# A four-layer graph kernel: neighbours centred in their sorting networks, networks in place, and small sums moved to TensorE

## The chip, the core and the metric

The kernel runs on one NeuronCore of a Trainium2 chip. A core has a matrix engine (TensorE, PE in the profile), a vector engine (VectorE, DVE), an activation engine (ScalarE, ACT), a general engine (GpSimd, POOL) and a queue engine for plain DMA transfers (SyncE, SP). They run in parallel and wait for each other through semaphores. The metric is the time on the device in microseconds (us), the median of several runs. The profile is one execution taken apart.

## The reference

Sixteen graphs of 1024 nodes with 64 features each; an adjacency matrix with random weights, about 16 neighbours to a node. Four layers, each a pre-normalised residual step `x = x + layer(relu(layernorm(x)))`:

```python
# layer 0:  h + messages, a tanh network
messages = einsum('bij,bjh->bih', adjacency, h)
dh = tanh(concat([h, messages]) @ W1 + b1) @ W2 + b2
# layer 1:  weighted mean over neighbours and self
A = edges + eye;  out = (A @ nodes) / A.sum(2)
# layer 2:  per node and channel, quantiles over the neighbours
nb = (adj > 0) & ~eye                     # rows with more than 10 neighbours lose some of them
removed = nb & do_dil & ((rank + 1) % skip == 0)
valid = where(removed | removed.T, 0, adj_with_self_loops) > 0
sv = sort(where(valid, x[:, None], big), axis=2);  m = valid.sum(-1)
for tau, wt in zip([.25, .5, .75], [.25, .5, .25]):
    pos = tau * (m - 1)                   # interpolated between sv[floor(pos)] and sv[ceil(pos)]
    agg += wt * quantile
y = relu((x + agg) @ W1 + b1) @ W2 + b2
# layer 3:  mean message
out = (A @ X / A.sum(1)) @ W_neighbors + X @ W_self + bias
```

## The kernel before

A graph's nodes lie on the 128 partitions in eight blocks. For layer 2 the kernel orders the 1024 nodes by their number of neighbours, m, cuts them into eight blocks of 128 and treats these in five groups (`GROUPS`): block 0 alone, block 1 alone, then three pairs. Every group has a capacity `cap` (38, 20, 18, 16, 13 places) and a lower bound `low` for m. For a group GpSimd gathers, place by place, one neighbour's feature row for every node of a block: one indirect DMA of 128 rows of 64 floats (line 1243, tile `raw`). How many places of a block are gathered whole stands in `PLACES`; the few rows of block 0 with more neighbours get theirs through three packed gathers (line 1224). Places beyond the neighbours are filled with zeros. VectorE then sorts each node's list per channel with an odd-even merge network: every step is a minimum or a maximum of two strided views, many comparators in one instruction (line 1285). The results of one layer go from `raw` to a second tile `other` or back, so that no step overwrites its own input; the home of every place is followed in `_program`, and comparators whose sources or targets lie in different tiles need instructions of their own. Comparators that no wanted place needs are dropped. At last each wanted place is multiplied by a weight per node (zero for places that a node's quantiles don't touch) and added up in `agg` (lines 1306 and 1308).

The rest of one graph: `adjacency` (transposes the matrix by TensorE, finds which neighbours go, ranks the nodes by m, writes keys to DRAM), `neighbour_lists` (gathers keys in node order on GpSimd, line 1064, and takes the neighbours in eights with MAX8, lines 1079 to 1095; then `index` and the weights), `layers` (layers 0 and 1 and the normalised input of layer 2), `gathers`, `sorts`, and `tail` (brings `agg` back to node order on GpSimd, line 1328, layer 2's two matrix products, layer 3).

A second, general path stands behind a test at the end and isn't taken with these inputs. These six are Python generators, and a small planner at build time interleaves them over the sixteen graphs. It keeps a clock for each engine (`clk`), advanced by rough costs that the generators state; a generator that yields a time is resumed when VectorE's clock has reached it; among those that are due the first in the list goes, so `sorts` comes last. The order on each engine is fixed by this; on the chip, semaphores hold each instruction until its inputs are there. GpSimd's gathers are charged 1.27 us each. `gathers(b)` for group k may start once `sort(b-1, k)` is done, since `raw` has one buffer for each group.

GpSimd is kept from running ahead of VectorE's plan by marks and gates. The planner lets VectorE write a mark (a one-element memset, line 889) whenever 4 us of its clock have gone by; before every fourth place of a group, GpSimd copies the latest mark (line 896, `gate`), and so waits until VectorE has passed it.

Small sums are VectorE's: the biases b02, b22 and b3 (lines 1154, 1344, 1363), the residuals (1163, 1365), the self term and the one of layer 1's denominator (1185, 1188) and the sum in front of layer 2's products (1332), each a 128x512 operation on one graph's nodes except for line 1185.

Of the kernel before, what the change touches and what calls it, by code (L numbers as in the profile page):

```python
# [17 lines left out]
P = 128  # L18
C = 64
# [18 lines left out]
GROUPS = [(0, 1, 38, 17), (1, 1, 20, 15), (2, 2, 18, 12), (4, 2, 16, 10), (6, 2, 13, 1)]  # L38

E_ID, E_ONE, E_CAP, E_LOW, E_CN, E_Q, E_END = 0, 128, 256, 264, 272, 280, 320  # L40
# [3 lines left out]
PLACES = [22, 20, 18, 17, 16, 14, 13, 12]  # L44
PACKS = [(22, 2, 64), (24, 4, 32), (28, 10, 12)]
# [3 lines left out]
def _span(cap, low):  # L49

    return (low - 1) // 4, -(-3 * (cap - 1) // 4)


def _network(cap, low):
# [16 lines left out]
    lo, hi = _span(cap, low)  # L71
    live, kept = set(range(lo, hi + 1)), []
    for layer in reversed(layers):
        layer = [(i, j, i in live, j in live) for i, j in layer if j < cap and (i in live or j in live)]
        for i, j, _, _ in layer:
            live |= {i, j}
        if layer:
            kept.append(layer)
# [3 lines left out]
def _patterns(items):  # L82


    left, out = set(items), []
    while left:
        best = None
        for x in sorted(left):
            steps = sorted({(y[2] - x[2], y[3] - x[3]) for y in left if y[:2] == x[:2] and y > x})

            def run(start, v):
                row = [start]
                while (z := (*x[:2], row[-1][2] + v[0], row[-1][3] + v[1])) in left:
                    row.append(z)
                return row

            for v in [None, *steps]:
                row = [x] if v is None else run(x, v)
                if best is None or len(row) > len(best[0]):
                    best = (row, x, [(len(row), *(v or (0, 0)))])  # L100
                for w in steps if v else []:
                    cover, m = list(row), 1
                    while all((z := (*x[:2], r[2] + m * w[0], r[3] + m * w[1])) in left and z not in cover
                              for r in row):
                        cover += [(*x[:2], r[2] + m * w[0], r[3] + m * w[1]) for r in row]
                        m += 1
                    if m > 1 and len(cover) > len(best[0]):
                        best = (cover, x, [(m, *w), (len(row), *v)])
        left -= set(best[0])
        out.append(best[1:])  # L110
    return out


def _program(cap, low):


    home, out = [0] * cap, []
    for layer in _network(cap, low):
        for greater in (True, False):
            items = [(home[i], home[j], i, j) for i, j, a, b in layer if (a if greater else b)]  # L120
            out += [(greater, p) for p in _patterns(items)]
        for i, j, _, _ in layer:
            home[i] ^= 1
            home[j] ^= 1
    lo, hi = _span(cap, low)
    return out, _patterns([(home[q], 0, q, q - lo) for q in range(lo, hi + 1)])


QT = sum((_span(cap, low)[1] + 1 - _span(cap, low)[0]) * n for _, n, cap, low in GROUPS)
# [584 lines left out]
def direct_path(ctx: ExitStack, tc: tile.TileContext, t: dict, out: bass.AP, flag):  # L714
# [25 lines left out]
    cap8, low8, cn8 = (cf[:, e:e + NB] for e in (E_CAP, E_LOW, E_CN))  # L740
# [30 lines left out]
    def along(name, src):  # L771
        w = const.tile([P, C], F32, name=name)
        nc.gpsimd.dma_start(w, bass.AP(tensor=src.tensor, offset=src.offset, ap=[[0, P], [1, C]]))
        return w[:, None, :].to_broadcast([P, NB, C])

    w01, w02 = weight("L0_gnn_W1", 2 * C), both_halves("L0_gnn_W2", C)
    b01, b02 = column("L0_gnn_b1", C, 2), along("b02", t["L0_gnn_b2"])
    w21, w22 = both_halves("L2_gnn_W1"), weight("L2_gnn_W2", P)
    b21, b22 = column("L2_gnn_b1", P), along("b22", t["L2_gnn_b2"])
    w3n, w3s = both_halves("L3_gnn_W_neighbors", C), both_halves("L3_gnn_W_self", C)  # L780
    b3 = along("b3", t["L3_gnn_bias"])
# [79 lines left out]
    def paired(h, dst):  # L861

        p = bank()
        for q in range(4):
            nc.tensor.transpose(p[:, q * P:(q + 1) * P], h[:, 2 * q:2 * q + 2, :].rearrange("p u c -> p (u c)"), identf)  # L865
# [4 lines left out]
    def per_node(p, lhs, w, n):  # L870

        o = NB // n * C
        for i in range(n):
            nc.tensor.matmul(p[:, i * o:(i + 1) * o], lhs[:, i * P:(i + 1) * P], w, start=True, stop=True)  # L874
        return p.rearrange("p (i c) -> p i c", c=C)
# [6 lines left out]
    marks, gates = [], []  # L882
# [3 lines left out]
    def mark():  # L886
        if not marks or clk.dve > marks[-1][0] + 4.0:
            t = slots[:, len(marks) % 8:len(marks) % 8 + 1]
            nc.vector.memset(t, 0.0)  # L889
            clk.dve += 0.06  # L890
            marks.append((clk.dve, t))

    def gate():
        if marks and gates[-1:] != marks[-1:]:
            gates.append(marks[-1])
            nc.gpsimd.tensor_copy(opened[:, len(gates) % 2:len(gates) % 2 + 1], marks[-1][1])  # L896
# [158 lines left out]
    def neighbour_lists(b):  # L1055
# [15 lines left out]
        total = sum(n * -(-cap // 8) * 8 for _, n, cap, _ in GROUPS)  # L1071
# [3 lines left out]
        for b0, n, cap, _ in GROUPS:  # L1075
# [25 lines left out]
        ts(index, found, -1.0, float(N), op0=ALU.mult, op1=ALU.add)  # L1101
        pack_d = dram.tile([len(PACKS), P], I32, name="pack_d")
        pack = nodes.tile([P, len(PACKS)], I32, name="pack")
        for l, (s0, ns, nn) in enumerate(PACKS):
            nc.sync.dma_start(pack_d[l, :ns * nn].rearrange("(n s) -> n s", s=ns), index[:nn, s0:s0 + ns])
        for l, (s0, ns, nn) in enumerate(PACKS):
            nc.sync.dma_start(pack[:ns * nn, l:l + 1], pack_d[l, :ns * nn].rearrange("(n o) -> n o", o=1))
# [6 lines left out]

        at = nodes.tile([P, 3, NB], F32, name="at")
        for k in range(3):
            ts(at[:, k], m, (k + 1) / 4, -(k + 1) / 4, op0=ALU.mult, op1=ALU.add)
        far = lists.tile([P, 3, QT], F32, name="far", bufs=1)
        o = 0
        for b0, n, cap, low in GROUPS:  # L1120
            lo, hi = _span(cap, low)
            k = hi + 1 - lo
            tt(far[:, :, o:o + k * n].rearrange("p t (q i) -> p t q i", i=n),
               cf[:, None, E_Q + lo:E_Q + hi + 1, None].to_broadcast([P, 3, k, n]),
               at[:, :, None, b0:b0 + n].to_broadcast([P, 3, k, n]), ALU.subtract)
            o += k * n
# [16 lines left out]
    def layers(b):  # L1143
# [10 lines left out]
        tt(x, x, b02, ALU.add)  # L1154
        yield after(0.7, pe=10.5, act=1.1)
# [5 lines left out]
        dh = per_node(bank(), th, w02, 4)  # L1161
        yield after(0, pe=1.3, act=2.1) + 2.8
        tt(x, x, dh, ALU.add)
        clk.dve += 0.7
        ha = nodes.tile([P, NB, C + 1], F32, name="ha")
        yield from preln(0, x, ha)
# [5 lines left out]
        for i in range(NB):  # L1172
            nc.tensor.transpose(p[:, i, :C + 1], nt[:, i * P:(i + 1) * P], identf[:C + 1, :C + 1])
# [11 lines left out]
        ts(den, p[:, :, C:C + 1], 1.0, None, op0=ALU.add)  # L1185
        nc.vector.reciprocal(den, den)
        o = mid(0, [P, NB, C])
        tt(o, p[:, :, :C], ha[:, :, :C], ALU.add)
        tt(o, o, den.to_broadcast([P, NB, C]), ALU.mult)
# [3 lines left out]
        clk.dve += 2.4  # L1193
        ha = nodes.tile([P, NB, C + 1], F32, name="h2", bufs=3)
        yield from preln(0, x, ha)
        nc.sync.dma_start(h_ds[b % 3][:N].rearrange("(i p) c -> p i c", p=P), ha[:, :, :C])
# [361 lines left out]
```

## Time and profile before

| quantity | value |
|---|---|
| time, median of 3 runs | 4355.45 us (4339.17 to 4363.22) |
| span of the profiled execution | 4291.0 us |
| DVE busy | 3488.6 us, 81% |
| POOL busy | 2727.1 us, 64% |
| PE / ACT busy | 1817.1 us (42%) / 1407.9 us (33%) |
| DMA moved | 366.81 MB, mean 85 GB/s |
| `agg` stores, first and last of the 16 | at 531.4 and 4225.3 us |

The busy time of an engine is the time in which at least one of its instructions was under way; where two overlap it is counted once. Rows that group instructions of a kind give the sum of their durations, so that on VectorE, where one instruction begins before its predecessor has ended, the rows add up to more than the engine's busy time. "Idle before" is what the engine stood still just ahead of the instructions of a row.

### The profile page before, as it was taken

The numbers are of one execution on the slowest core, as the hardware profiler recorded it, in microseconds if no ns is written. First come the engines' busy times: TensorE is split into PE (matmuls) and PEld (weight loads), VectorE is DVE, ScalarE is ACT, GpSimd is POOL, SyncE is SP. The second block draws the span as 40 slices with busy tenths as digits, with TensorE's granted clock in tenths as the row PEclk, the third lists the DMA queues.
The fourth block names the chain that finished last, engine by engine and source line by source line (L and its number), as shares of the span: only waits on it lengthen the run. The fifth ranks groups of instructions, "written<-read, shape, count | busy, mean of one in ns | idle before, by whom it ended". The sixth has DMA issues, their size and how long they took to land.

```text
span 4291.0 us, 34027 instructions
## 1 busy us (share of the span) xinstructions
PE 1817.1 (42%) x7875; PEld 884.0 (21%) x7875; DVE 3488.6 (81%) x10253; ACT 1407.9 (33%) x2594; POOL 2727.1 (64%) x2804
## 2 busy tenths in 40 slices
PE   6542545244353544434454343445434354532012
PEld 3312222121221212122121212213121221311000
DVE  2547868979798988979897897989889798989974
ACT  5533433232332424334242333424243342411000
POOL 1265767577676666866666586666758666676850
PEclk9665866566566766756676675667667576765555
DMA  2323332232423324242342424233242433323121
GB/s 91 109 77 81 83 111 58 83 92 67 118 71 102 103 67 106 64 126 70 92 114 61 109 67 121 75 92 109 51 124 67 111 85 87 94 45 105 41 44 48
DMA packets 240213, 366.81 MB, mean 85 GB/s; under 512 B 127472, under 2 KB 129248, under 8 KB 240000
## 3 DMA queue, kind: packets, MB, share of 16 engines
q1 hardware_dynamic: 155760, 254.99, 17.5%
q0 software_dynamic: 84096, 109.00, 14.5%
q8 instruction: 64, 1.05, 0.1%
q14 instruction: 149, 1.22, 0.1%
q10 hardware_dynamic: 144, 0.56, 0.0%
HBM read 249.54 MB, written 114.81 MB: 85 GB/s over the span
## 4 chain that ended last, share of the span: by engine, by line
DVE 54%; another core or an unknown queue 12%; POOL 9%; issue 9%; PE 7%; ACT 5%; DMA 3%; DVEq 0%; POOLq 0%; ACTq 0%
DVE other L1285 15%; DVE raw L1285 13%; POOL raw L1243 7%; DVE agg L1308 5%; DVE most L1093 5%; POOL res L1328 2%; DVE found L1079 2%; PE pt L858 2%; PE pt L874 1%; DVE half L1308 1%; ACT nb L932 1%; DVE k L1088 1%; DVE found L1095 1%; DMA k<-keys_d,node 1%
## 5 line engine op out<-in xcount | busy, mean ns | idle before, releaser
L1243 POOL DMA_INDIRECT raw<-h_d,index x2112 | 2288.6, 1084 | 670.4 <-issue 571.9
L1285 DVE TENSOR_TENSOR other<-raw 128x128 f32<-128x128 f32 (+7 forms) x1488 | 761.9, 533 | 81.4 <-remote 31.5
L1285 DVE TENSOR_TENSOR raw<-other 128x256 f32<-128x256 f32 (+10 forms) x1424 | 677.8, 489 | 12.8 <-issue 7.3
L858 PE MATMUL pt<-adjt,ha 128*65 128x512 f32 (+1 forms) x1024 | 498.2, 649 | 243.6 <-issue 88.7
L925 PE MATMUL pt<-ef,a 128*128 128x128 f32 x1024 | 238.6, 410 | 519.7 <-ACT adjt L926 345.9
L896 POOL COPY gate<-mark 1x1 f32<-1x1 f32 x364 | 109.8, 302 | 477.1 <-DVE mark L889 472.5
L925 PEld LDWEIGHTS pt<-ef,a 128*128 128x128 f32 x1024 | 191.3, 217 | 560.6 <-ACT adjt L926 378.2
L967 PE MATMUL pt<-eh,nbt 128*128 128x512 f16 (+3 forms) x1024 | 211.7, 365 | 206.8 <-ACT nbt L956 168.1
L1093 DVE MAX8 most<-k 128x8 uint16<-128x1024 uint16 x224 | 275.1, 1228 | 16.7 <-DVE k L1088 8.6
L858 PEld LDWEIGHTS pt<-adjt,ha 128*65 128x65 f32 (+1 forms) x1024 | 150.7, 151 | 571.8 <-issue 513.1
L1064 POOL DMA_INDIRECT k<-keys_d,node x128 | 127.0, 992 | 215.2 <-DVE node L1049 121.0
L859 ACT COPY big<-pt 64x1024 f32<-64x1024 f32 (+1 forms) x32 | 32.2, 1007 | 636.3 <-remote 362.3
L1285 DVE TENSOR_TENSOR raw<-other,raw 128x128 f32<-128x128 f32 (+5 forms) x560 | 196.3, 357 | 54.7 <-remote 45.4
L1000 ACT ACTIVATE nb<-pt 128x1024 f16<-128x1024 f32 x128 | 130.7, 1021 | 315.2 <-issue 126.6
L932 ACT ACTIVATE nb<-nb 128x512 f16<-128x512 f16 x256 | 159.5, 627 | 207.8 <-DVE nb L918 134.9
L1285 DVE TENSOR_TENSOR other<-raw,other 128x256 f32<-128x256 f32 (+4 forms) x592 | 206.5, 353 | 19.0 <-remote 13.9
L1328 POOL DMA_INDIRECT res<-agg_d,pos x128 | 141.0, 1102 | 107.1 <-issue 106.5
L1285 DVE TENSOR_TENSOR raw<-raw,other 128x256 f32<-128x256 f32 (+3 forms) x608 | 202.7, 338 | 2.1 <-issue 2.0
L1018 PE MATMUL pt<-spread,ef 128*128 128x512 f32 x64 | 61.1, 1055 | 335.7 <-DVE spread L1016 334.9
L865 PE MATMUL pt<-ef,res 128*128 128x128 f32 x64 | 17.4, 427 | 433.8 <-DVE res L1332 163.3
L1079 DVE MAX8 found<-k 128x8 f32<-128x1024 f16 x128 | 156.4, 1222 | 47.8 <-DMA k<-keys_d,node 47.8
L1285 DVE TENSOR_TENSOR other<-other,raw 128x256 f32<-128x256 f32 (+3 forms) x576 | 192.1, 337 | 2.1 <-issue 2.1
(167 smaller groups left out, 4162.1 us busy)
## 6 DMA issues: line engine op xcount, KB each, us to landing
a<-in_adj_dram SPq DMA_DIRECT2D x64, 1024.0 KB
adjt_d<-adjt SPq DMA_DIRECT2D x64, 1024.0 KB
at<-adjt_d SPq DMA_DIRECT2D x128, 512.0 KB
raw<-h_d,index POOLq DMA_INDIRECT x2112
keys_d<-nb SPq DMA_DIRECT2D x64, 512.0 KB
x<-in_x_dram SPq DMA_DIRECT2D x16, 256.0 KB
h_d<-h SPq DMA_DIRECT2D x16, 256.0 KB
agg_d<-agg SPq DMA_DIRECT2D x16, 256.0 KB
```

The costliest lines, as they stand in the source:

```text
L858: nc.tensor.matmul(p[p0:p0 + n, s], h[:, j, :n], adjt[:, j, s], start=j == 0, stop=j == NB - 1)
L925: nc.tensor.transpose(p[:, u * P:(u + 1) * P], a[:, j * P:(j + 1) * P], identf)
L932: act(nb[:, i, s], nb[:, i, s], AF.Copy, accum_out=mn[:, q, i:i + 1])
L967: nc.tensor.matmul(p[:, o:e], nbt[:, j, :], stair[:, :e - o], start=j % 4 == 0, stop=j % 4 == 3)
L1000: act(nb[:, i, :], p, AF.Relu)
L1064: nc.gpsimd.indirect_dma_start(k, None, g["keys_d"], bass.IndirectOffsetOnAxis(ap=g["node"][:, i:i + 1], axis=0))
L1079: nc.vector.max(out=found[:, o:o + 8], in_=src)
L1093: nc.vector.max(out=most, in_=less.bitcast(U16))
L1243: nc.gpsimd.indirect_dma_start(raw[:, s, i * C:(i + 1) * C], None, h_ds[b % 3], bass.IndirectOffsetOnAxis(ap=g["index"][:, at:at + 1], axi ...
L1285: tt(to, v0, v1, ALU.max if greater else ALU.min)
L1308: nc.vector.scalar_tensor_tensor(to, v, wq, to, op0=ALU.mult, op1=ALU.add)
L1328: nc.gpsimd.indirect_dma_start(res[:, i, :], None, g["agg_d"], bass.IndirectOffsetOnAxis(ap=g["pos"][:, i:i + 1], axis=0))
```

## The change

Five things are meant to take work off VectorE and GpSimd.

1. **Centred neighbours.** A node's m neighbours are put in the middle of the capacity: missing places are filled half with a very large number and half with zero (features are not negative), so the sorted list lies about the centre whatever m is, and the quantiles of all m fall on fewer places. `_wanted` lists them; the network is cut out of the larger one at an offset (`above`). Padding costs two extra rows of the feature table in DRAM (row 0 of zeros, row N+1 of `BIG`), and ScalarE's fill of the unused places has two values.
2. **Networks in place.** The step's target may be one of its own sources, if both views are the same places. A string for each group says, layer by layer and pair of homes, which results move to the other tile (`b`, `i`, `j`), chosen ahead of time so that few instructions are needed.
3. **Tighter groups.** The capacities of groups 1 to 4 are one place smaller, and so is every entry of `PLACES`.
4. **Biases and residuals by TensorE.** They become matrix products with ones or with the identity that accumulate in the same PSUM tile; where x itself is needed again, ScalarE copies it out.
5. **Marks only where GpSimd waits.** A mark is written at the place where a gate is issued, and the generator of the gathers is resumed 5 us instead of 3 us ahead of GpSimd's planned clock.

```diff
-GROUPS = [(0, 1, 38, 17), (1, 1, 20, 15), (2, 2, 18, 12), (4, 2, 16, 10), (6, 2, 13, 1)]
+GROUPS = [
+    (0, 1, 38, 17, 0, "b b bj b i j j j ji i j ij i i jb i i bj bi b b"),
+    (1, 1, 19, 15, 0, "b jb b i j j j jb j i ji j i jb b"),
+    (2, 2, 17, 12, 15, "b b b b b b i ib i iib bjb j j i b"),
+    (4, 2, 15, 10, 0, "b jb bj b j ji b i bj b"),
+    (6, 2, 12, 1, 0, "b b b b j b b b ji b"),
+]
+BIG = 1e30
...
-PLACES = [22, 20, 18, 17, 16, 14, 13, 12]
-PACKS = [(22, 2, 64), (24, 4, 32), (28, 10, 12)]
+PLACES = [21, 19, 17, 16, 15, 13, 12, 11]
+PACKS, NPACK = [(0, 0, 21, 2, 64), (1, 0, 23, 1, 32), (1, 32, 24, 4, 24), (2, 0, 28, 10, 12)], 3
...
+def _wanted(cap, low):
+    places = set()
+    for m in range(low, cap + 1):
+        above = (cap + 1) // 2 - (m + 1) // 2
+        places |= {above + k * (m - 1) // 4 for k in (1, 2, 3)} | {above - k * (1 - m) // 4 for k in (1, 2, 3)}
+    return sorted(places)
...
-    def paired(h, dst):
+    def paired(hs, dst):
         p = bank()
         for q in range(4):
-            nc.tensor.transpose(p[:, q * P:(q + 1) * P], h[:, 2 * q:2 * q + 2, :].rearrange("p u c -> p (u c)"), identf)
+            for e, h in enumerate(hs):
+                nc.tensor.matmul(p[:, q * P:(q + 1) * P], h[:, 2 * q:2 * q + 2, :].rearrange("p u c -> p (u c)"), identf,
+                                 start=e == 0, stop=e == len(hs) - 1)
...
-    def per_node(p, lhs, w, n):
+    def per_node(p, lhs, w, n, bias=None, x=None):
...
+        if bias is not None:
+            nc.tensor.matmul(v, onesf[:1], bias, start=True, stop=False)
+        if x is not None:
+            nc.tensor.matmul(v, identf, x, start=False, stop=False)
...
-    def mark():
-        if not marks or clk.dve > marks[-1][0] + 4.0:
-            t = slots[:, len(marks) % 8:len(marks) % 8 + 1]
-            nc.vector.memset(t, 0.0)
-            clk.dve += 0.06
-            marks.append((clk.dve, t))
...
     def gate():
-        if marks and gates[-1:] != marks[-1:]:
-            gates.append(marks[-1])
-            nc.gpsimd.tensor_copy(opened[:, len(gates) % 2:len(gates) % 2 + 1], marks[-1][1])
+        if not marks or clk.dve > marks[-1] + 4.0:
+            k = len(marks)
+            nc.vector.memset(slots[:, k % 8:k % 8 + 1], 0.0)
+            clk.dve += 0.15
+            nc.gpsimd.tensor_copy(opened[:, k % 2:k % 2 + 1], slots[:, k % 8:k % 8 + 1])
+            marks.append(clk.dve)
...
-        ts(index, found, -1.0, float(N), op0=ALU.mult, op1=ALU.add)
+        nc.vector.tensor_copy(to[:, 1], of[:, 1])
+        ts(none, of[:, 0], 0.0, float(N + 1), op0=ALU.is_equal, op1=ALU.mult)
+        tt(to[:, 0], none, of[:, 0], ALU.add)
...
+        ts(above[:, 0], m, 1.0, None, op0=ALU.add)
+        ts(above[:, 1], above[:, 0], 1, None, op0=ALU.arith_shift_right)
+        tt(s[:, 0], half8, above[:, 1], ALU.subtract)
+        ts(s[:, 1], m, -1.0, None, op0=ALU.add)
...
-        tt(x, x, b02, ALU.add)
-        yield after(0.7, pe=10.5, act=1.1)
+        yield after(0, pe=10.5, act=1.1)
...
-        dh = per_node(bank(), th, w02, 4)
+        p = per_node(bank(), th, w02, 4, b02, x)
+        nc.scalar.copy(x, p)
         yield after(0, pe=1.3, act=2.1) + 2.8
-        tt(x, x, dh, ALU.add)
-        clk.dve += 0.7
         ha = nodes.tile([P, NB, C + 1], F32, name="ha")
-        yield from preln(0, x, ha)
+        yield from preln(0, p, ha)
...
-        for i in range(NB):
-            nc.tensor.transpose(p[:, i, :C + 1], nt[:, i * P:(i + 1) * P], identf[:C + 1, :C + 1])
+        for q in range(0, NB, 4):
+            nc.tensor.matmul(p[:, q:q + 4, :C + 1], identf, ha[:, q:q + 4, :], start=True, stop=False)
+            for i in range(q, q + 4):
+                nc.tensor.matmul(p[:, i, :C + 1], nt[:, i * P:(i + 1) * P], identf[:C + 1, :C + 1], start=False,
+                                 stop=i == q + 3)
...
-        ts(den, p[:, :, C:C + 1], 1.0, None, op0=ALU.add)
-        nc.vector.reciprocal(den, den)
+        nc.vector.reciprocal(den, p[:, :, C:C + 1])
...
-        tt(o, p[:, :, :C], ha[:, :, :C], ALU.add)
-        tt(o, o, den.to_broadcast([P, NB, C]), ALU.mult)
+        tt(o, p[:, :, :C], den.to_broadcast([P, NB, C]), ALU.mult)
...
                 if s % 4 == 3:
-                    yield clk.pool - 3
+                    yield clk.pool - 5
...
-        tt(res, res, ha[:, :, :C], ALU.add)
...
-        paired(res, rt)
+        paired((ha, res), rt)
...
-        y = per_node(bank(), h1, w22, 8)
+        y = per_node(bank(), h1, w22, 8, b22)
...
-        tt(o, y, b22, ALU.add)
-        tt(o, o, mask[:, b, :, None].to_broadcast([P, NB, C]), ALU.mult)
+        tt(o, y, mask[:, b, :, None].to_broadcast([P, NB, C]), ALU.mult)
...
-        paired(ha, ht)
-        zs = per_node(bank(), ht, w3s, 4)
-        tt(x, x, b3, ALU.add)
-        yield after(0.7, pe=3, lat=0.5)
-        tt(x, x, zs, ALU.add)
-        clk.dve += 0.7
+        paired((ha,), ht)
+        nc.scalar.copy(x, per_node(bank(), ht, w3s, 4, b3, x))
+        yield after(0, pe=3, act=0.6, lat=0.5)
```

The counts of instructions that follow from the program of the two kernels, for all sixteen graphs:

| instructions | before | after |
|---|---|---|
| network steps on VectorE | 5248 | 3184 |
| elements per partition in these steps, sum | 1,435,648 | 1,283,072 |
| weighted sums that accumulate (line 1308 before) | 1504 | 1024 |
| marks on VectorE / gates on GpSimd | 800 / 364 | 293 / 293 |
| gathers of one place on GpSimd | 2112 | 1984 |
| ScalarE fills / copies of x | 64 / 0 | 96 / 32 |

## The prediction

> **What bounds the kernel now.** First the page's busy times, then its chain of waits, then the costliest groups.
>
> ```profile
> PE 1817.1 (42%) x7875; PEld 884.0 (21%) x7875; DVE 3488.6 (81%) x10253; ACT 1407.9 (33%) x2594; POOL 2727.1 (64%) x2804
> ...
> DVE 54%; another core or an unknown queue 12%; POOL 9%; issue 9%; PE 7%; ACT 5%; DMA 3%; DVEq 0%; POOLq 0%; ACTq 0%
> ...
> L1243 POOL DMA_INDIRECT raw<-h_d,index x2112 | 2288.6, 1084 | 670.4 <-issue 571.9
> ...
> L896 POOL COPY gate<-mark 1x1 f32<-1x1 f32 x364 | 109.8, 302 | 477.1 <-DVE mark L889 472.5
> ```
>
> VectorE is busiest and holds over half of the chain. GpSimd is nearer to it than 64% says: between two gathers it stands still without a releaser ("issue"), 571.9 us in all, so a gather occupies it for (2288.6 + 571.9) / 2112 = 1.354 us. With the issue gaps of its other indirect DMAs (about 35 + 38 + 14 us by the list of waits, without one long wait of 68 us) GpSimd needs 2727 + 572 + 87 = 3386 us, 211.6 us a graph. It has time to spare: it waits 472.5 us at its gates for VectorE.
>
> A graph takes (4225.3 - 531.4) / 15 = 246.3 us, from the first and last store of `agg`. The busy time by stretch gives the steady state:
>
> ```profile
> 535.00:3862.00 3327.00, 1472.57 (x6403) 714.06 (x6404) 2848.98 (x8298) 1135.71 (x2092) 2257.85 (x2312) 0.67 0.34 88
> ```
>
> The columns after the length are PE, weight loads, VectorE, ScalarE and GpSimd. 3327 us are 13.5 graphs: VectorE is busy 210.9 us a graph and idle 35.4. This idle time is many short waits; the largest in the list of VectorE's waits over this stretch are gathers that have not landed (78 us, as "remote"), the key gathers (42 us), and results of TensorE and ScalarE (den 37, gone 36, spread 27).
>
> What a network step costs is read from the order of time on VectorE, not from the group's mean, since steps overlap:
>
> ```profile
> 1523.85 0.28 DVE L1285 TENSOR_TENSOR raw<-raw,other 128x128 f32<-128x128 f32 x1
> 1524.05 0.28 DVE L1285 TENSOR_TENSOR other<-other,raw 128x128 f32<-128x128 f32 x1
> 1524.37 0.42 DVE L1285 TENSOR_TENSOR other<-raw,other 128x256 f32<-128x256 f32 x1
> 1524.72 0.42 DVE L1285 TENSOR_TENSOR raw<-other,raw 128x256 f32<-128x256 f32 x1
> 1525.05 0.42 DVE L1285 TENSOR_TENSOR raw<-other 128x256 f32<-128x256 f32 x1
> 1525.39 0.42 DVE L1285 TENSOR_TENSOR other<-other,raw 128x256 f32<-128x256 f32 x1
> ```
>
> Columns: start and duration in us, then the instruction. The starts lie 0.20 us apart for 128 elements and 0.34 for 256, though the durations are 0.28 and 0.42: about 1.04 ns an element and a fixed 0.07 us.
>
> **What the Trainium skill says.** "Vector Engine (DVE) Microarchitecture Reference", section "Measured stream behaviour on trn2", gives 1.0417 ns per column and about 75 ns per instruction after queue overlap; the starts above agree (0.07 us). So both a smaller count and fewer elements pay. "SBUF — State Buffer", section "SBUF: two separate sides", says that VectorE and GpSimd share a port pair that one of them holds for a whole instruction, and that descriptors for GpSimd's DMA must wait for it. Here a gather takes 0.968 us at the median, 1.084 on the mean and 2.75 at most; long ones lie beside 1024-wide steps, which fits but doesn't prove that cause.
>
> **The change, part by part.**
>
> VectorE, network (in place, centred, tighter): 5248 - 3184 = 2064 instructions at 0.07 us = 144 us; 1,435,648 - 1,283,072 = 152,576 elements at 1.04 ns = 159 us. Together 303 us. With fewer steps to a layer, more steps read what the step before them wrote and can't overlap it: by the two programs 41 instead of 34 a graph, at 0.08 us under 10 us in all, which I neglect.
>
> Weighted sums: 480 fewer. Thirteen of them in a row take 2.70 us in the order of time, 0.208 each: 100 us.
>
> Small sums: seven 128x512 operations a graph go, with rows of 10.9, 10.8, 10.2, 11.1, 11.1, 10.9 and 10.9 us, and line 1185 with 2.6: 78.5 us, less some 8 us of overlap: 70 us. Marks: 507 fewer at 59 ns: 30 us. Added: three half-width operations for `index` instead of one (16 x (3 x 0.2 - 0.26), 5 us) and four small ones at 0.17 us, 11 us.
>
> Sum for VectorE: 303 + 100 + 70 + 30 - 16 = 487 us, 30.4 a graph, nearly all on the limiting engine.
>
> GpSimd: 128 gathers at 1.354 us = 173 us, and 71 gates at 0.302 = 21 us: 194 us, 12.1 a graph, to 199.5 us. The packed gathers stay three a graph. While VectorE sets the pace this is worth nothing of its own; it keeps GpSimd from becoming the limit.
>
> TensorE and ScalarE get work that I cost at nothing in throughput: a graph gains three bias products and two identity products of 128x512 (1.055 us each by the row of that shape, line 1018), four 128x128 (0.43) and two of 260 columns, about 8 us on an engine busy 114 us of 246; ScalarE gains 2 copies of 0.6 us and two fills. What counts is latency where VectorE waits for PSUM: about 2.1 us ahead of layer 0's sum, 1.2 ahead of `den`, 2.8 ahead of `y`, and the planner's charges for TensorE there are unchanged. Ends: 0 (the planner has other work for VectorE there: the old sum of layer 0, line 1163, waited in 2 of 16 graphs) and 6 us a graph. I take 1.5, 24 us in all.
>
> Gates: GpSimd now waits for a mark written at the gate's own place in VectorE's order, where before it was up to 4 us old, and its generator is resumed 5 instead of 3 us ahead. Age and lead balance: about 5 us before and after. Behind a late gate stand the gathers, and for them the sorts. Ends: 0 and a doubling of the 472 us; I take 0.
>
> GpSimd's margin falls from 246.3 - 211.6 = 34.7 us a graph to about 16, so sorts will find their gathers late more often. Before, network steps lost 172 us to idle time ahead of them by their six rows. Ends: 0 and twice as much (+172); I take 32 us.
>
> Likeliest: 4291 - 487 + 24 + 32 = 3860 us for a profiled execution. The median of the runs was 64 us above the profiled span before; kept, this gives about **3920 us**. A graph would take near 220 us.
>
> **Rivals.** (A, 0.65) as above, 3820 to 4020 with the bounds of the waits that can be hidden.
>
> (B, 0.15) GpSimd becomes the limit, with losses in proportion. Before, a graph took 246.3 us with 211.6 of GpSimd work; if the same factor, 1.164, holds for 199.5 us, a graph takes 232.2 and the gain is 14.1 x 16 = 226 us: **4130 us**. For it: the planner charges 1.27 us for a gather that takes 1.354, so GpSimd lags behind a plan in which both engines are now nearly equal. Against: the gates' 472 us show GpSimd waiting, not VectorE.
>
> (C, 0.15) the idle time shrinks too, as a plan in balance leaves VectorE holes that cover the short waits. Then only GpSimd's work limits, some 204 us a graph: (246.3 - 204) x 16 = 677 us less, **3680 us**. Against: the 35 us of idle time come from waits for TensorE, ScalarE and landings which the change does not shorten.
>
> (D, 0.05) slower: fresh marks hold GpSimd behind every stall of VectorE. If its waits double to 945 us, GpSimd needs 3192 + 945 = 4137 us, to which the some 200 us before its first gather and 140 after its last come: about **4500 us**.
>
> **How the numbers follow.** The time is A's. The range runs from C's 3690 to short of B's, 4090, with D and the upper part of B left out. Faster by over 0.5%: A, B and C nearly whole, 0.94; within 0.5%: a B that loses more, 0.02; slower: 0.04.
>
> **What would show it.** VectorE busy near 3000 us and network steps with starts that follow the same 0.07 us and 1.04 ns; GpSimd's gate waits falling well below 472 us, since its margin halves; the stores of `agg` 215 to 222 us apart. The prediction is wrong if VectorE's idle time a graph leaves 30 to 42 us, if the mean gather gets slower than 1.084 us because VectorE holds the port for more of the time, or if waits for line 1217's PSUM operand or the `y` of layer 2 grow by more than 6 us a graph.

## The result, and the profile after

| | before | changed |
|---|---|---|
| time, median of 4 runs each, same chip | 4347.31 us (4312.79 to 4363.22) | 4036.73 us (4017.74 to 4053.95) |
| ratio | 1 | 0.9295, 95% interval 0.9223 to 0.9366 |
| span of the profiled execution | 4291.0 us | 4035.0 us |
| VectorE busy / idle | 3488.6 / 802.4 us | 3070.5 / 964.5 us |
| `agg` stores, first to last | 246.3 us a graph | (3969.1 - 475.9) / 15 = 232.9 us a graph |

The change gains 311 us where 427 were forecast (4347 to 3920). First the page of the changed kernel: the engines, the chain of waits, and the two GpSimd groups shown of the kernel before.

```profile
PE 2059.4 (51%) x8483; PEld 1008.6 (25%) x8483; DVE 3070.5 (76%) x7173; ACT 1426.3 (35%) x2658; POOL 2592.2 (64%) x2608
...
DVE 51%; PE 13%; another core or an unknown queue 12%; issue 10%; ACT 6%; DMA 4%; POOL 4%; DVEq 0%; SPq 0%; ACTq 0%; POOLq 0%
...
L1274 POOL DMA_INDIRECT raw<-h_d,index x1984 | 2164.2, 1091 | 575.4 <-issue 548.5
...
L917 POOL COPY gate<-mark 1x1 f32<-1x1 f32 x293 | 96.6, 330 | 477.8 <-DVE mark L915 457.6
```

VectorE lost 418 us of work and still heads the chain, but TensorE's share rose from 7% to 13%, and VectorE's busy share of the span fell from 81 to 76%: it stands idle more, not less. GpSimd's gates still wait 457.6 us, so GpSimd isn't the limit. The steady stretch says the same:

```profile
535.00:3600.00 3065.00, 1647.65 (x6811) 801.73 (x6812) 2469.52 (x5785) 1146.14 (x2140) 2099.43 (x2100) 0.68 0.33 93
```

3065 us are 13.16 graphs of 232.9 us: VectorE is busy 187.7 us a graph (210.9 before) and idle 45.2 (35.4 before). What it waits for, from the list of its waits (us in total, times, longest), kernel before and then changed:

```profile
DVE x L1163 <- PE pt L874: 39.7, 2, 21.5
DVE den L1185 <- PE pt L1173: 37.4, 11, 8.8
...
DVE mid L1344 <- PE pt L874: 8.6, 1, 8.6
...
DVE mid L1344 <- remote: 7.1, 2, 4.1
```

```profile
DVE mid L1360 <- PE pt L899: 141.2, 11, 24.1
DVE stat L846 <- ACT x L1192: 77.5, 3, 30.4
...
DVE den L1217 <- PE pt L1204: 71.7, 6, 26.0
DVE den L1217 <- remote: 66.5, 5, 20.2
```

Line 1360 reads the `y` of layer 2 (line 1344 before), line 846 the sum of layer 0 through ScalarE's copy (line 1163 before), line 1217 the denominator (line 1185 before). All three wait for TensorE. The wait for `y` rose from 15.9 us to 141.2, that for `den` from 37.4 to 154.3, in which 16.1 us are put down to "issue".

### The profile page after: what moved, and what is told of

Read it like the earlier page. It is cut to its first block, busy times and chain, and to the rows that moved or that the text cites. A ratio compares the mean times of both kernels' runs of the same rounds, so it can differ in the third digit from the quotient of the medians.

```text
span 4035.0 us, 32061 instructions
## 1 busy us (share of the span) xinstructions
PE 2059.4 (51%) x8483; PEld 1008.6 (25%) x8483; DVE 3070.5 (76%) x7173; ACT 1426.3 (35%) x2658; POOL 2592.2 (64%) x2608
## 4 chain that ended last, share of the span: by engine, by line
DVE 51%; PE 13%; another core or an unknown queue 12%; issue 10%; ACT 6%; DMA 4%; POOL 4%; DVEq 0%; SPq 0%; ACTq 0%; POOLq 0%
DVE other L1307 14%; DVE raw L1307 14%; PE pt L875 6%; DVE most L1115 4%; POOL raw L1274 4%; DVE agg L1326 2%; DVE found L1101 2%; ACT adjt L1210 2%; PE pt L899 1%; DMA adjt_d<-adjt 1%; DVE nb L940 1%; ACT nb L954 1%; DVE k L1110 1%; DMA raw<-h_d,index 1%
## 5 line engine op out<-in xcount | busy, mean ns | idle before, releaser
L1274 POOL DMA_INDIRECT raw<-h_d,index x1984 | 2164.2, 1091 | 575.4 <-issue 548.5
L1307 DVE TENSOR_TENSOR other<-raw 128x512 f32<-128x512 f32 (+11 forms) x816 | 536.1, 688 | 43.9 <-DMA raw<-h_d,index 27.3
L917 POOL COPY gate<-mark 1x1 f32<-1x1 f32 x293 | 96.6, 330 | 477.8 <-DVE mark L915 457.6
L1307 DVE TENSOR_TENSOR raw<-other 128x512 f32<-128x512 f32 (+10 forms) x464 | 356.4, 792 | 6.5 <-DVE other L1307 1.1
L948 ACT COPY adjt<-pt 128x512 f32<-128x512 f32 x256 | 138.9, 583 | 242.1 <-PE pt L947 80.6
L1307 DVE TENSOR_TENSOR raw<-other,raw 128x640 f32<-128x640 f32 (+3 forms) x448 | 216.9, 495 | 7.7 <-remote 1.9
L1307 DVE TENSOR_TENSOR raw<-raw,other 128x128 f32<-128x128 f32 (+7 forms) x496 | 212.4, 437 | 12.2 <-remote 4.4
L1307 DVE TENSOR_TENSOR other<-other,raw 128x128 f32<-128x128 f32 (+4 forms) x448 | 201.8, 461 | 8.2 <-remote 2.3
L993 ACT ACTIVATE gone<-pt,sf 128x512 f16<-128x512 f32 x256 | 162.8, 691 | 112.2 <-remote 46.5
L1018 PE MATMUL pt<-eh,gone 128*128 128x128 f16 x1024 | 132.7, 261 | 124.5 <-DVE gone L1003 37.8
L978 ACT COPY nbt<-pt 128x1024 f16<-128x1024 f16 x128 | 128.5, 1015 | 146.6 <-remote 106.4
```

Of the source, the lines that this page charges most:

```text
L948: nc.scalar.copy(adjt[:, 4 * q:4 * q + 4, i * P:(i + 1) * P], p.rearrange("p (u m) -> p u m", m=P))
L993: act(gone[:, i, s], p[:, s], AF.Abs, bias=sf[:, 2 + q, i:i + 1], scale=2.0)
L1018: nc.tensor.matmul(p[:, d], gone[:, j, i * P:(i + 1) * P], big_i, start=False, stop=j == 4 * q + 3 and i // 4 != q)
L1274: nc.gpsimd.indirect_dma_start(raw[:, s, i * C:(i + 1) * C], None, h_ds[b % 3], bass.IndirectOffsetOnAxis(ap=g["index"][:, at:at + 1], axi ...
L1307: tt(view(two[to], *((i, vi) if greater else (j, vj)), w), view(two[s], i, vi, w), view(two[u], j, vj, w), ALU.max if greater else ALU.min)
```

## Experiments

Each kernel is timed beside the kernel before on the same chip. The chip of the result above is called A here; the experiments ran on three different chips, B, C and D, four kernels on each. Whether A is one of C and D isn't on record. The kernel before took 4347, 3963, 4294 and 4290 us on A to D. Ratios are to these, with 95% intervals. The changed kernel itself wasn't run on B; there e3, which differs from it only in the marks and the lead of the gathers (part 5), stands in for it.

### Chip B: one part undone at a time

**e1_sums_on_vector**: part 4 undone.

```diff
-        p = per_node(bank(), th, w02, 4, b02, x)
-        nc.scalar.copy(x, p)
+        dh = per_node(bank(), th, w02, 4)
+        tt(x, x, dh, ALU.add)
... and so for b22, b3, the self terms, both residuals and the sum ahead of layer 2's products
```

> The changed kernel with its fourth part undone: biases, residuals and layer 1's self term are VectorE operations again and TensorE only transposes; networks, groups and marks stay as changed. Theory 1 (VectorE's idle time grew because it waits for the longer chains and the fuller queue of TensorE): VectorE's busy time rises by about 70 us to 3140, TensorE's falls by about 240 to 1820, and VectorE's idle time falls from 964 by 100 us or more, so that the time is 4036 + 70 - 100 or less: 4010 or below. Theory 2 (the idle time comes from the thinner margin to GpSimd and the gates): the idle time stays near 960 and the time rises by the 70 us, to about 4105.

**e2_ping_pong**: part 2 undone, every result of a step moves to the other tile.

```diff
-        for (s, u), flip in zip(pairs, flips, strict=True):
+        for s, u in pairs:
+            flip = "b"
```

> The changed kernel with the networks not in place: every result moves to the other tile, as before the change; the comparators and their elements are the changed kernel's (80,192 elements a graph), the instructions are 324 a graph instead of 199. By the price of 0.07 us an instruction alone VectorE's busy time rises by 2000 x 0.07 = 140 us. If steps in place lose their overlap with the step before (79 of 199 read or overwrite what the step before wrote or read, here 53 of 324), 26 x 16 x 0.1 = 42 us of it are given back, so about 100 us: 3170 us busy. VectorE as the limit: time 4036 + 100 = 4136. If VectorE is not the limit the time rises by less than 40 us.

**e3_old_marks**: part 5 undone.

```diff
+    def mark():
+        if not marks or clk.dve > marks[-1][0] + 4.0:
+            nc.vector.memset(t, 0.0)
...
-                    yield clk.pool - 5
+                    yield clk.pool - 3
...
+            mark()
```

> The changed kernel with the marks as before the change: one each 4 us of the planned clock, gates copy the latest mark, gathers resumed 3 us ahead. Theory (marks are only their instructions): some 450 more memsets at 59 ns, 27 us, time about 4060. Rival (a mark at the gate's own place makes GpSimd wait for VectorE's stalls): gate waits fall well below 458 us and the time falls under 4000.

**e4_no_gates**: no gates and no marks; only buffers and indices hold GpSimd back.

```diff
     def gate():
+        return
```

> The changed kernel without marks and gates: GpSimd gathers as soon as its data and buffers are there. Theory (GpSimd has a margin, VectorE and its waits set the time): the 458 us of gate waits turn up as waits for index tables, buffers and keys instead, and the time stays within 1% of 4036. Rival (the gates are what holds the chain): the time falls by 60 us or more, below 3975. Third case (gates keep GpSimd's work in the planner's order of urgency, and gathers ahead of time meet wide VectorE steps): mean gather above 1.12 us and the time above 4080.

| chip B | us | ratio | VectorE busy / idle | gate waits |
|---|---|---|---|---|
| kernel before | 3962.54 | 1 | no profile | |
| e1, sums on VectorE | 3663.01 | 0.9247 (0.9227 to 0.9266) | 3135.4 / 523 | 77.8 |
| e2, ping-pong | 3697.46 | 0.933 (0.9314 to 0.9345) | 3173.0 / 527 | 179.3 |
| e3, old marks | 3665.7 | 0.925 (0.9235 to 0.9266) | 3075.9 / 590 | 71.7 |
| e4, no gates | 3619.82 | 0.9134 (0.9117 to 0.9151) | 3069.2 / 552 | none |

In place is worth some 0.8% (e2 beside e3, whose networks are those of the change; their marks differ). e2's busy time of 3173.0 us is the 3170 that was expected from the price of an instruction and the number of dependent steps; of the 97 us more work than in e3, 32 show in the time. e1 and e3 differ in part 4 and in the marks, and come out alike: the sums on TensorE saved 60 us of VectorE's work and added 67 us of idle time. Without the gates (e4) the kernel is 46 us or 1.3% faster than with the old ones (e3). The old marks add little work to VectorE. Their group in e3:

```profile
L915 DVE MEMSET mark<- x681: 59/59/59, 1.3 to 3653.5; 1x1 f32 x171
```

388 marks more than the change has, at 59 ns each, are 23 us by the row; VectorE's busy time is 5.4 us longer than the changed kernel's on chip A, 3075.9 against 3070.5. Nearly all of a mark lies beside a step that runs anyway. Parts 1 and 3 were not undone in any run.

### Chip C: why VectorE stands idle more

**e5_changed_again**: the changed kernel, as this chip's reference.

> The changed kernel itself once more, beside the kernel before on this chip, since the four experiments so far ran on a chip on which the kernel before took 3963 us instead of 4347. If the ratio belongs to the kernels it is 0.93 here too (3683 us where before takes 3963) and the experiments' ratios of 0.925 (sums on VectorE), 0.933 (ping-pong), 0.925 (old marks) and 0.913 (no gates) can be set against it. If the slower chip had cost the changed kernel more, it is 0.92 or below.

**e6_charges**: the planner's charges for TensorE raised to what the profile after shows, so that VectorE gets other work ahead of those waits.

```diff
-        yield after(0, pe=1.3, act=2.1) + 2.8
+        yield after(0, pe=6.0, act=2.7) + 2.8
...
-        yield after(0, pe=2.2, act=1.5) + 3.2
+        yield after(0, pe=7.0, act=1.5) + 3.2
... and four more
```

> The changed kernel with the planner's charges for TensorE set to what its products take in the changed kernel's trace (messages 16 us instead of 10.5, layer 0's sum 6.0 instead of 1.3, y 7.0 instead of 2.2, layer 3's self term 5.2 instead of 3, the transposes in pairs 2.1 each instead of 1.5). No instruction differs, only their order. Theory (VectorE stands at PSUM operands because the plan resumes it too early): its waits for den, y and the first sum of layer 1's norm fall by 60 us or more in all and the time falls by 30 us or more against the changed kernel. Rival (the waits are set by TensorE's queue, and what is put off there comes back later): the time stays within 20 us.

**e7_copy_later**: ScalarE's copy of x after layer 0 is issued behind the pre-norm instead of ahead of it.

```diff
-        nc.scalar.copy(x, p)
         yield after(0, pe=1.3, act=2.1) + 2.8
...
         yield from preln(0, p, ha)
+        nc.scalar.copy(x, p)
```

> The changed kernel with ScalarE's copy of x out of PSUM issued after the norm's reads of the same tile instead of before them, so that VectorE's reduction need not wait for the copy. Theory (the copy lies in the chain): VectorE's wait of layer 1's norm for the copy (77 us in 3 waits on the first chip) turns into a wait for TensorE and falls by some 16 x 0.6 = 10 us or more; time 0 to 20 us less. Rival (the copy only happens to end last): no difference.

**e8_spaced_steps**: the steps of a network reordered, so that 53 instead of 79 a graph follow directly on a step that they depend on.

```diff
-    return out, [(home[q], q, e) for e, q in enumerate(_wanted(cap, low))]
+    return _spaced(out), [(home[q], q, e) for e, q in enumerate(_wanted(cap, low))]
```

> The changed kernel with the same network steps, each network's steps reordered at build time so that fewer follow directly a step whose result they read or whose operand they overwrite: 53 of 199 a graph instead of 79. Theory (a dependent step loses its overlap with the step before, some 0.1 us): VectorE's busy time falls by 26 x 16 x 0.1 = 42 us, and the time by 20 to 42 us. Rival (steps in place cost no overlap): VectorE's busy time stays within 10 us.

| chip C | us | ratio | VectorE busy |
|---|---|---|---|
| kernel before | 4293.98 | 1 | no profile |
| e5, changed kernel | 3969.68 | 0.9266 (0.9225 to 0.9308) | 3070.5 |
| e6, higher charges | 4110.56 | 0.9607 (0.9553 to 0.9661) | 3071.5 |
| e7, copy later | 3985.97 | 0.9287 (0.9254 to 0.932) | 3071.4 |
| e8, spaced steps | 4006.47 | 0.9328 (0.9278 to 0.9378) | 3037.4 |

e6 loses 141 us against e5, which neither expectation had. It did shorten the waits that it was meant for: in all, that for `den` fell from 153.7 us in e5 to 67.4 and that for `y` from 139.0 to 47.9. But what it held back came late elsewhere. Its waits of VectorE, then of GpSimd:

```profile
DVE other L1307 <- DMA raw<-h_d,index: 149.6, 22, 25.0
...
DVE den L1217 <- PE pt L1204: 37.0, 2, 25.1
```

```profile
POOL packed L1255 <- DMA pack<-pack_d: 312.5, 22, 36.6
```

The longest is now the network waiting for gathers, and the gathers wait for the index lists of their own graph (312.5 us; 50.8 us in e5). e7 changed no time that can be measured (the intervals overlap): the wait for the copy, 39.5 us in e5, gave way to waits for TensorE or without a releaser, 70.8 us in all, so it didn't set the pace. e8 takes 33 us off VectorE's busy time, which shows that dependent steps do cost, but the time is no shorter: its interval overlaps that of e5. VectorE's work alone does not set the time.

### Where the late results come from

The share of "another core or an unknown queue" in the chain was no part of my prediction. This program runs on one core, so the name is only where the profile finds no releaser. It is 12% in both kernels on chip A, and 0 in all four on chip B, at equal work (VectorE busy 3070.5 on A, 3075.9 in e3 on B). So the raw semaphore events of the traces were read: for each signal of TensorE, how long after the end of its last recorded instruction it comes. On chip B no signal in any of the four kernels is later than 1.3 us, the program's last 15 us left aside; in e4 98% come within 30 ns. In the changed kernel on A 61% do, and on A, C and D many come over 3 us late:

| stretches with TensorE's signal over 3 us late | number | sum, us | longest | VectorE idle inside them, us |
|---|---|---|---|---|
| chip A, before | 36 | 312 | 21.9 | 174 |
| chip A, changed | 53 | 481 | 21.6 | 255 |
| chip C, changed (e5) | 56 | 451 | 22.1 | 229 |
| chip D, changed (e12) | 49 | 452 | 22.8 | 233 |
| chip D, sums on VectorE (e11) | 52 | 445 | 21.2 | 203 |
| chip D, no gates (e10) | 78 | 1019 | 49.6 | 717 |
| chip D, no gates, sums on VectorE (e9) | 74 | 879 | 45.9 | 576 |
| chip B, e1 to e4 | 0 | 0 | | 0 |

Not every signal is in the table, for the traces of A, C and D lack some: by TensorE's records 1032 are due in the changed kernel, and 870 stand in the trace on A, 873 on C and 887 on D, while e3 on B has 1032 of 1034; a wait that ended on a signal that isn't there may stand under another name. The records themselves are complete (8483 of TensorE in e4 as in e10).

The late stretches are also tied to places in the program. TensorE's records come in the same order in the changed kernel on A, C and D; counted again for this, A has 55 such stretches, C 56 and D 50, and 37 of A's and 38 of D's begin right behind the same record as one of C's. In the kernel before, 12 of the 36 lie behind line 858's products, each 9.6 to 11.0 us long, one each in 12 of the graphs. So something in the program seems to set them off, and chip B doesn't answer to it. In the 10 us ahead of a late stretch TensorE's records are denser than ahead of its other gaps over 3 us: busy 76 to 80% against 59 to 60% in the changed kernel on A, C and D. That dense work is the cause isn't shown.

### Chip D: gates and sums, two by two

**e9_sums_vector_no_gates** (edits of e1 and e4 together), **e10_no_gates_again** (e4's kernel), **e11_sums_vector_again** (e1's kernel), **e12_changed_beside** (the changed kernel).

> The changed kernel with two things at once: part 4 undone (the small sums on VectorE again) and no gates and marks (GpSimd's gathers run as early as their buffers and indices allow). Theory 1 (the two effects are separate: the sums on TensorE gain nothing because what VectorE saves in work it loses in waits for PSUM, and the gates cost some 1.3%): about 0.912 of the kernel before, within 0.004 of the run without gates. Theory 2 (without gates VectorE is the only limit, so its 65 us of extra busy time count in full): 0.927, slower than the run without gates by 1.5%. Theory 3 (without gates the planner's order is not held by GpSimd, and the waits for PSUM are the largest that are left, so taking them away gains now): 0.900.

> The changed kernel without gates and marks, on the same chip as the other runs of this call. Theory 1 (gates hold GpSimd for nothing): 1.3% faster than the changed kernel, as measured on another chip against the other variants there, about 0.914 of the kernel before. Theory 2 (on a chip with more stalls the gates protect the order, and GpSimd's gathers compete with the other DMA traffic): no gain over the changed kernel, 0.927.

> The changed kernel with part 4 undone (the small sums on VectorE), now beside the changed kernel on the same chip. Theory 1 (part 4 gains nothing, since VectorE's saved work turns into waits for PSUM): within 0.5% of the changed kernel, about 0.926. Theory 2 (my prediction: 70 us less work for VectorE, 24 us more waits, so part 4 gains 46 us or 1.1%): 0.938. Theory 3 (the waits outweigh the work): 0.918.

> The changed kernel itself, as the common reference of this call: 0.9266 to 0.9295 of the kernel before by its two measurements so far.

| chip D (before: 4290.31 us) | gates | no gates |
|---|---|---|
| sums on TensorE | e12: 3970.28 us, 0.924 (0.9202 to 0.9278) | e10: 4698.57 us, 1.0931 (1.0857 to 1.1005) |
| sums on VectorE | e11: 3995.93 us, 0.9322 (0.9282 to 0.9362) | e9: 4557.96 us, 1.0633 (1.0558 to 1.0708) |

None of my theories for e9 and e10 had this: the kernel that was the fastest on chip B is the slowest here, 18% above the changed kernel. With gates, part 4 gains 26 us on this chip (the intervals just part); without them it loses 141. e11 and e12 differ in part 4 alone: it takes VectorE's busy time from 3140.6 to 3070.4 us and adds 59 us of idle time in the profiled executions.

The profiles of the same kernel without gates on B (e4) and D (e10) can be laid side by side. The chains of waits, e4 and then e10:

```profile
DVE 47%; POOL 18%; PE 14%; issue 9%; ACT 6%; DMA 6%; DVEq 0%; SPq 0%; POOLq 0%; ACTq 0%
```

```profile
DVE 37%; another core or an unknown queue 25%; PE 14%; issue 10%; ACT 7%; DMA 3%; POOL 2%; DVEq 0%; SPq 0%; ACTq 0%; POOLq 0%
```

ScalarE's waits, e4 and then e10. All these lines take a result of TensorE out of PSUM. In e4 the longest waits have TensorE as their releaser; in e10 lines 979, 1023 and 949 have none that the profile finds:

```profile
ACT big L876 <- PE pt L875: 478.7, 32, 23.2
ACT nb L1023 <- PE pt L1019: 332.8, 51, 28.9
```

```profile
ACT nbt L979 <- remote: 310.5, 26, 29.1
ACT nb L1023 <- remote: 233.9, 32, 41.0
ACT adjt L949 <- remote: 230.8, 30, 54.6
```

One such stretch of e10 in order of time (start, duration, instruction, in brackets the idle time before it):

```profile
2612.00 3.25 PE L899 MATMUL pt<-L_gnn_W,big 128*128 128x64 f32 x14 [4.90 <-ACT big L1357]
...
2615.05 1.91 PE L948 MATMUL pt<-ef,a 128*128 128x128 f32 x8
...
2656.27 0.94 POOL L1275 DMA_INDIRECT raw<-h_d,index  x1 [0.30 <-issue]
2666.56 0.58 ACT L949 COPY adjt<-pt 128x512 f32<-128x512 f32 x1 [54.61 <-remote]
...
2667.20 1.11 PE L948 MATMUL pt<-ef,a 128*128 128x128 f32 x4 [50.24 <-ACT adjt L949]
...
2670.02 0.20 DVE L854 RECIPROCAL stat<-stat 128x8 f32<-128x8 f32 x1 [81.33 <-ACT stat L852]
```

TensorE's records end at 2616.96. Its next two signals come at 2661.6 and 2666.5 in the semaphore events. The Trainium skill, "Perfetto Trace Analysis", section "Tensor Engine Instruction (MATMUL, LD_WEIGHTS)", says how both can be true: the end of a TensorE record is computed from the size of the instruction, and the semaphore is updated only once PSUM has the data. The trace agrees that the two can part: here they lie 45 and 50 us apart, where nothing is late 14 ns. Until then ScalarE waits for the first transposes, TensorE for a free PSUM buffer, VectorE for ScalarE, while GpSimd goes on gathering. In e10 VectorE's idle time is 1641 us, against 552 in e4.

What makes TensorE late on A, C and D and never on B stays open. Three thoughts were tried on the traces and explain too little. The DMA engines: the stretches of e10 over 5 us in which TensorE, VectorE and ScalarE all stand mostly have only gathers under way, at 0.1 to 0.25 of the engines' time. Instruction loading: of the 199 packets of the instruction queues in e10 only 12 start within its 78 late stretches, and of TensorE's 110 gaps over 6 us in the changed kernel on A only about a tenth end within 4 us after one. The granted clock is at half for 91% of the late time in e10 and for 70% of its span, but for 60% of the span of e4 too, where nothing is late. The Trainium skill, "TensorE: Matmul & The Clock Gate", section "Seeing it yourself", warns that clock events on trn2 can be wrong and that the clock has been seen stuck at a quarter for over 50 us. The length would fit; but no record here is below a half, and the 5.2 us of work in the stretch shown, recorded at half clock, would take about 10 us at a quarter (an estimate from the two records), not 50. Nor do the traces tell why the gates matter so much: GpSimd is busy in 687 of the 1019 us in e10 (67%, and 51% of its span), and in 294 of the 452 us in e12 (65%, as in its span). Whether gathers lengthen the lateness or merely go on through it wasn't tried.

## Why the prediction was right in direction and short in size

The saving came from where it was looked for: VectorE's work, the network first, with GpSimd following. What failed is the term for waits. Two of my own signs of being wrong came: VectorE's idle time a graph is 45.2 us, outside 30 to 42, and the waits for `den` and `y` grew by more than 6. A third came by a hair, with a mean gather of 1.091 us against 1.084; its cause wasn't tested, and the section of the Trainium skill that I named for it, "SBUF: two separate sides", puts a condition that I left out: descriptors wait for VectorE's two-port modes, while operations with two SBUF inputs hold off only those of GpSimd that read SBUF. The time lies between the likeliest case and rival B, 17 us above the upper end that I gave the likeliest case. B's mechanism didn't come: GpSimd waits 457.6 us at its gates. On the profiled span the balance is

- forecast: VectorE's work -487, waits +24 and +32, in all -431;
- measured: work 3070.5 - 3488.6 = -418, idle time +162, in all -256.

**Network, 303 forecast, 258 measured** (the time that its steps add to what ran before them, 1927 to 1669 us). The counts and both prices of independent steps were right; the step that failed is the one that I neglected, "41 instead of 34 a graph". I counted only steps that read what the step before wrote. A step in place also overwrites what the step before it may still be reading, and that one waits too: by the two programs 44 steps a graph follow such a step before (34 + 10) and 79 after (41 + 38). The order of time of the changed kernel shows it:

```profile
1527.43 0.55 DVE L1307 TENSOR_TENSOR raw<-raw,other 128x384 f32<-128x384 f32 x1
1527.45 0.06 DVE L915 MEMSET mark<- 1x1 f32 x1
1528.02 0.56 DVE L1307 TENSOR_TENSOR raw<-raw,other 128x384 f32<-128x384 f32 x1
1528.61 1.15 DVE L1307 TENSOR_TENSOR other<-other,raw 128x384 f32<-128x384 f32 x2
```

Starts 0.59 us apart at a duration of 0.55: no overlap. With the program's list of steps laid on the trace, every pair of neighbouring steps can be sorted. From start to start, less 1.04 ns an element, an independent step takes 0.07 us in both kernels, one that reads what the step before wrote 0.19, and one that overwrites what the step before reads 0.19 too. So both kinds cost 0.12 us more, where I had 0.08 for one of them. The 35 more a graph make 560 in all, an estimate of up to 67 us from these spacings; the sum fell short by 45. The Trainium skill, "Vector Engine (DVE) Microarchitecture Reference", section "Measured stream behaviour on trn2", gave me some 75 ns an instruction after queue overlap; for independent steps the trace agrees (0.07), for dependent ones the measured spacing decides, and it is wider. e8, with 26 fewer a graph, got 33 us of it back.

**Weighted sums, 100 forecast, 97 measured** (counted as for the network). **Small sums, 70 forecast, 70 measured** on one chip (VectorE busy in e11 and e12: 3140.6 and 3070.4); e1 on B, 3135.4, is 65 above the changed kernel on A. The 16 us added were not separated.

**Marks, 30 forecast, about 7**: 5.4 us for 388 of them in e3, in proportion for 507. I priced by the row's duration what lies beside other instructions.

**TensorE, "about 8 us a graph", measured 242 us or 15.1 a graph** (11.8 to 13.1 for part 4 alone, by e1 and e3 and by e11 and e12). The price that I took, 1.055 us for 128x512, is that of one record, and a float32 product leaves two. The groups of TensorE after, mean ns of a record behind the busy time:

```profile
L895 PE MATMUL pt<-b,ef 1*128 1x512 f32 x96 | 80.5, 930 | 0.1
...
L897 PE MATMUL pt<-x,ef 128*128 128x512 f32 x64 | 51.5, 898 | 0.0
```

48 products with a bias are 96 records, 1.68 us a product; 32 with the identity are 64 records, 1.61. A transpose had left one record; as a product that adds up it leaves two (line 1173 before: 128 records; line 1204: 256). The counts beside the rows tell it.

**Waits for PSUM, 24 us forecast with 96 as the far end.** For `den` they grew by 117 us, for `y` by 125, for the sum of layer 0 by 38 (39.7 to 77.5). My own bound of 6 us a graph was passed by the first two (7.3 and 7.8). Part of it was repaid: idle time ahead of network steps fell from 172 to 98 us, where I had added 32, and the waits for `res` (73.5 us) are gone. On balance +162 us. 81 of these lie in the stretches in which TensorE's signal is late (174 to 255), which I had not priced; they needn't all be part 4's, since on chip D e12 has only 30 us more than e11 there. On chip B, where nothing is late, part 4 still added 67 us of idle time (e3 beside e1, whose marks differ). So part 4, which I had put at 70 - 24 = 46 us, gave nothing on chip B and 26 us on chip D. The +162 isn't split further.

**Gates, 0 forecast, "falling well below 472".** Whether the new marks and lead cost time beside the old isn't shown: no two runs differ in them alone. The sign I named did not come: 472.5 and 457.6. On chip B gates wait only 71.7 to 179.3 us. A gate waits for VectorE, so where VectorE stands waiting for TensorE the gates show it as theirs; that fits the two chips, but wasn't separated. GpSimd's own terms were right: 1984 gathers, mean 1.091 us (1.084 before).

**The offset.** I carried over 64 us between the profiled span and the median. After the change it was 2 us (4036.73 and 4035.0). By luck that hid some 60 us of the error on the span, 3860 against 4035.0, which is 175 us.

**Period.** 215 to 222 us between `agg` stores were forecast and 232.9 came. Rival B's 232.2 is met by coincidence, since its mechanism is absent. On chip B e1 has (3595.6 - 435.6) / 15 = 210.7.

## What to carry to other kernels

Price an instruction that loses independence from its neighbour at its whole duration, and count overwriting as well as reading; price a product by all the records that it leaves. Work moved from the busiest engine to a less busy one is only gained if the new producer is earlier than its reader: here 60 us of sums became 67 us of waiting on chip B, and 70 became 59 on chip D. Waits moved by a plan can come back elsewhere: e6 took 177 us off two waits and lost 141 us. A throttle between engines that looks like pure waiting (472 us at the gates) should be tried on more than one chip before it is taken out: doing so gained 1.3% on one and cost 18% on another.

## What the runs showed of the hardware that was not expected

The same program with the same VectorE time ran at 3620 us on one chip and at 4699 on another (e4, e10), and with gates the kernels were 8 to 10% slower on A, C and D than on B (before: 3963 against 4290 to 4347 us). The difference that the traces show is in TensorE's signals, 7 to 9 us late at the median of the late stretches and up to 49.6, though the page books TensorE as done. On A, C and D two thirds of the late stretches begin behind the same instructions, on B none does. How much of the slowness they make isn't settled: VectorE is idle in them for 717 us of the 1079 by which e10 is longer than e4. The ends of TensorE's records are modelled; "another core or an unknown queue" in the chain of a single-core program was the place where it showed, and about half of that share lies in the late stretches (253 of 474 us in the changed kernel on A). And a VectorE step that overwrites what its neighbour reads waits as long as one that reads what its neighbour wrote, 0.19 us against 0.07 where the two are independent.
